# Group norms in the stage ahead, an image's chunks loaded as they are last read, two tiles' weighing on VectorE and smaller clears, in a four-layer image network

## The chip, the cores and the metric

The kernel runs on one core of a Trainium2 chip. The metric is the device time of one execution in microseconds (us). Engines are named as in the profile: PE is TensorE (PEld its weight loads), DVE VectorE, ACT ScalarE, POOL GpSimd, and SP the engine that issues most DMAs.

## The reference, cut to what matters

Four images of 56 x 56 positions and 128 channels go through four layers. Each layer takes the group-normed image (32 groups of 4 channels, statistics over all positions of one image) and adds its result to the image.

```python
x = x + L0(group_norm(x))   # window attention (7x7 windows, shifted by 3) + full attention + MLP
x = x + L1(group_norm(x))   # mamba: projection, 3x3 conv, selective scan in four directions, gated output
x = x + L2(group_norm(x))   # deformable 3x3 convolution
x = x + L3(group_norm(x))   # as L0, other weights
```

So nothing of a layer can start on an image before the last position of the layer ahead of it is known: the norm's statistics need them all. Different images are independent of one another.

## The kernel before, in words

An image is held as a tile of 128 channels (partitions) by 3136 positions, in seven chunks of 448. Two such tiles, `xs[b % 2]`, hold the images at work; image b+2 is loaded over image b when b is finished. `run` sets the order of the stages:

- b=0: attention L0(0), its MLP and the mamba convolution, scan(0), `mamba_out`(0);
- b=1: attention L0(1), MLP and convolution (1) woven with the deformable layer of image 0, scan(1), `mamba_out`(1), then attention L3(0) and `mlp` L3(0);
- b=2: the same with L0(2), deformable(1), `mamba_out`(2), L3(1);
- b=3: L0(3), deformable(2), `mamba_out`(3), attention L3(2), `mlp` L3(2) woven with deformable(3), and last attention L3(3) and `mlp` L3(3).

Statistics of chunk c (`stats`, line 124) are made on DVE as the chunk gets its final value, and `group_norm` (lines 142 to 159) turns them into a mean and 1/deviation for each channel: an aggregate on DVE (L146), a matmul that averages groups (gn_pm, L148), three small DVE operations, a second matmul (gn_pv, L155), a square root on ACT with a load of its function table (L157), and a reciprocal on DVE (L158).

An attention has two parts. The windows part works on eight bands of eight windows each, called tiles. For tile t, `tokens` (L241 to L249) gathers the band into xw, normed, in three to six pieces (on DVE for the first two tiles, on POOL for the others); `project` makes pq and pk on PE (L254); `queries`, `keys` and `values` bring them to qp, kb and v on ACT; `scores` makes pss on PE (L279) and takes the maximum away on DVE (L285, L286); `exponentials` is on ACT; `normalize` sums and inverts on DVE and multiplies to pz on POOL (L297, one product for each half of the partitions); `turn`, `turned`, `weigh` and `out` follow on PE and ACT. xw, qp, kb and pz exist twice and have padding that must be zero, so POOL clears them whole once in each attention (L243 and L249). The order of these steps, tile by tile, is written by hand. The main part, full attention over 3136 positions, follows it (maxima, L371 to L376; scores, L552; exponentials, L553; values, L579) and needs three tiles that POOL clears once in an attention: the ends of ks and qs (L344, L345) and mx (L359).

`mlp` runs over the seven chunks, an iteration for each n, with steps of several chunks in each: `center` (a matmul, a square on ACT, and on POOL the sum that reads x for the last time, L690), `spread`, `scale`, `shift`, `hidden` (PE and Gelu on ACT), `result` (py, L717) and `store` (L721). In layer L3 the store writes into x, and `finish` (L1519 to L1523) sends that chunk out and then loads the next image's chunk into the same place:

```python
    def finish(self, b, x, cols):
        self.nc.sync.dma_start(self.out[b][:, cols], x[:, cols])
        if b + 2 < self.B:
            self.nc.sync.dma_start(x[:, cols], self.x_in[b + 2][:, cols])
```

The statistics of images 2 and 3 are all made at the head of `run`'s loop, those of image 1 in `mamba_out`(0), each behind image 0's of the same chunk.

`mamba_out` (from L1207) does the last steps of the mamba layer by chunk: the scan's result ya less its mean (L1222, L1229), squares, a root (Ln and Exp on ACT), the gate z from the normed image (L162, L1240), and pmo (L1267), which `store` (L1270) adds to x. Ahead of it POOL's last work is the scan's sum hs (L1135).

Of the kernel before, what the change touches and what calls it, by code (L numbers as in the profile page):

```python
# [10 lines left out]
F32 = mybir.dt.float32  # L11
# [3 lines left out]
ALU = mybir.AluOpType  # L15
# [4 lines left out]
P = 128  # L20
HW = 56
L = HW * HW
CH = 448
# [55 lines left out]
class _Net:  # L79
    def __init__(self, ctx, tc, x, packs, out):  # L80
        self.tc, self.nc, self.x_in, self.out, self.packs = tc, tc.nc, x, out, packs
        self.B = x.shape[0]
        nc = self.nc
        wp = ctx.enter_context(tc.tile_pool(name="weights", bufs=1))
        self.keep = wp
        self.w = {}
        self.xs = [wp.tile([P, L], F32, tag=f"x{i}", name=f"x{i}") for i in range(2)]
        for c in range(NCK):
            cols = slice(c * CH, (c + 1) * CH)
            nc.sync.dma_start(self.xs[0][:, cols], x[0][:, cols])  # L90
        for layer, queue in (("L0", nc.scalar), ("C", nc.scalar), ("L1", nc.sync), ("L3", nc.sync)):
            self.load(layer, wp, queue)
        c = self.w["C"]
        self.ident, self.gmat = c["ident"], c["gmat"]
        self.ones = {1: c["ones1"], 2: c["ones2"]}
        self.center = {1: (c["center1"],), 2: (c["center2"], c["others2"])}
        self.sel = wp.tile([P, KB], F32R, tag="sel", name="sel")
        nc.vector.memset(self.sel.bitcast(F32), 0.0)
        for h in range(NH):
            nc.vector.memset(self.sel[h * DK : h * DK + 2, :].bitcast(F32), 1.0)  # L100
        self.ident2 = wp.tile([64 + NX, NX], F32R, tag="ident2", name="ident2")
        nc.vector.memset(self.ident2.bitcast(F32), 0.0)
        for k in (0, 64):
            nc.vector.tensor_copy(self.ident2[k : k + NX, :], self.ident[:NX, :NX])
        self.all1 = wp.tile([P, P], F32, tag="all1", name="all1")
        nc.vector.memset(self.all1, 1.0)
        self.one32 = self.all1[:, :DK]
        self.eps = wp.tile([P, 1], F32, tag="eps", name="eps")
        nc.vector.memset(self.eps, 1e-5)
        self.any = wp.tile([P, 1], F32, tag="any", name="any")  # L110
        self.sts = [wp.tile([P, NCK, 6], F32, tag=f"gn_st{i}", name=f"gn_st{i}") for i in range(2)]
        self.dpool = ctx.enter_context(tc.tile_pool(name="tables", bufs=1, space=DRAM))


# [26 lines left out]
    def group_norm(self, b, sb, bank):  # L141
        nc = self.nc
        st = self.sts[b % 2]
        self.table_of(AF.Sqrt)
        mv = sb.tile([P, 2], F32, tag="gn_mv", name="gn_mv")
        nc.vector.bn_aggr(mv, st.rearrange("p c s -> p (c s)"))  # L146
        pm = bank("gn_pm")
        nc.tensor.matmul(pm[:, 0:1], lhsT=self.gmat, rhs=mv[:, 0:1], start=True, stop=True)  # L148
        mean = sb.tile([P, 1], F32, tag="gn_mean", name="gn_mean")
        nc.vector.tensor_copy(mean, pm[:, 0:1])  # L150
        dv = sb.tile([P, 1], F32, tag="gn_dv", name="gn_dv")
        nc.vector.tensor_sub(dv, mv[:, 0:1], mean)
        nc.vector.scalar_tensor_tensor(dv, dv, dv, mv[:, 1:2], ALU.mult, ALU.add)
        pv = bank("gn_pv")
        nc.tensor.matmul(pv[:, 0:1], lhsT=self.gmat, rhs=dv, start=True, stop=True)  # L155
        rstd = sb.tile([P, 1], F32, tag="gn_rstd", name="gn_rstd")
        nc.scalar.activation(rstd, pv[:, 0:1], AF.Sqrt, bias=self.eps)  # L157
        nc.vector.reciprocal(rstd, rstd)  # L158
        return mean, rstd

    def gn_apply(self, out, x, gn):
        self.nc.vector.tensor_scalar(out, x, gn[0], gn[1], ALU.subtract, ALU.mult)  # L162
# [58 lines left out]
    def windows(self, layer, x, x1, gn, sb, bank):  # L221
# [18 lines left out]

        def tokens(t):  # L241
            if t < 2:
                nc.gpsimd.memset(xw[t], 0.0)  # L243
            xv = xw[t % 2][:, :, :n1].rearrange("p w (r c) -> p w r c", c=WS)
            for (a, r, c), at in self.window_pieces(order[t]):
                (nc.vector if t < 2 else nc.gpsimd).tensor_scalar(xv[:, a, r, c], self.piece(img, at), gn[0], gn[1], ALU.subtract, ALU.mult)
            if t < 2:
                for z in (qp, kb, pz):
                    nc.gpsimd.memset(z[t], 0.0)  # L249

        def project(t):
            for n in "qk":
# [38 lines left out]
        def normalize(t):  # L291
            s, d = later.pop(("s", t)), later.pop(("m", t))
            nc.vector.tensor_reduce(d, s, AX.X, ALU.add)
            nc.vector.reciprocal(d, d)  # L294
            for j in range(2):
                rows = slice(64 * j, 64 * j + 64)
                nc.gpsimd.tensor_tensor(pz[t % 2][rows, :, j, :n1], s[rows], d[rows, :, None].to_broadcast([64, ng, n1]), ALU.mult)  # L297

        def turn(t):
            for r in range(NPR):  # L300
# [28 lines left out]
    def attention(self, layer, b, x1, oT, sb):  # L329
# [11 lines left out]
        qs = sb.tile([P, LP], F32, tag="qs", name="qs")  # L341
        nm = sb.tile([P, L], F32R, tag="nm", name="nm")
        va = sb.tile([P, NKB, P], F32, tag="va", name="va")
        nc.gpsimd.memset(ks[:, L:], 0.0)  # L344
        nc.gpsimd.memset(qs[:, L:], 0.0)  # L345

        def part(c):
            return slice(c * CH, (c + 1) * CH)
# [7 lines left out]
        size = {g[0]: len(g) for g in groups_of}  # L356
        early = (NCK, NCK, NCK, NCK, NCK - 1, 1)
        mx = sb.tile([P, len(blocks), NH, NMX], F32, tag="mx", name="mx")
        nc.gpsimd.memset(mx, -3.0e38)  # L359
        used = {}  # L360

        xn = oT
        with tc.manual_schedule():
# [35 lines left out]

            with tc.tile_pool(name="ap_sb", bufs=2) as tb, tc.tile_pool(name="ap_ps", bufs=8, space=PSUM) as ps:  # L400
                bank = lambda name: ps.tile([P, 512], F32, tag="mm", name=name)
                of_windows = self.windows(layer, x, x1, self.group_norm(b, tb, bank), tb, bank)
                self.table_of_both()
                ln = {}

# [51 lines left out]
                for name in ("tokens", "project", "queries", "keys", "values"):  # L457
                    do(name, 0)
                do("tokens", 1)
                for u in range(NWIN + 1):  # L460
                    if u != 1:
                        do("scores", u)
# [206 lines left out]
    def mlp(self, layer, b, x1, oT, last, alone):  # L669
# [3 lines left out]
        with tc.tile_pool(name="mlp", bufs=2) as sb, tc.tile_pool(name="mlp_ps", bufs=1, space=PSUM) as ps:  # L673
            bank = lambda name, tag="mm": ps.tile([P, 512], F32, tag=tag, name=name, bufs={"mm": 6 if alone else 3, "pc": 2 if alone else 1}[tag])
            x2, m = x1, {}

            def cols(n):
                c = (n + 3) % NCK
# [7 lines left out]
            def center(n):  # L686
                (m["pc", n],) = self.ln_center([x2[:, cols(n)]], lambda name: bank(name, "pc"))
                m["sq", n] = sb.tile([P, 2, CH], F32, tag="ln_sq", name="ln_sq")
                nc.scalar.activation(m["sq", n][:, 0, :], m["pc", n][:, :CH], AF.Square)
                nc.gpsimd.tensor_add(x2[:, cols(n)], x2[:, cols(n)], x[:, cols(n)])  # L690

            def spread(n):
                sq = m["sq", n]
# [24 lines left out]

            def store(n):
                del m["h", n]  # L720
                nc.vector.scalar_tensor_tensor(x[:, cols(n)], m.pop(("py", n))[:, :CH], w["b2"], x2[:, cols(n)], ALU.add, ALU.add)  # L721
                if last:
                    self.finish(b, x, cols(n))
                else:
                    self.stats(b, (n + 3) % NCK)

# [12 lines left out]
            for n in range(-1, NCK):  # L739
                if do(hidden, n, (0, 1)):  # L740
                    yield 1.8
                do(scale, n + 1)
                if do(center, n + 2):
                    yield 0.9
                if do(hidden, n, (2, 3)):
                    yield 1.8
                do(shift, n + 1)
                if do(residual, n + 4):
                    yield 0.9
                if do(spread, n + 2):  # L750
                    yield 0.9
                if do(result, n, (0, 1)):
                    yield 1.8
                if do(result, n, (2, 3)):
                    yield 1.8
                do(store, n)


    def mamba_prepare(self):
# [450 lines left out]
    def mamba_out(self, b, ya, gn):  # L1210
# [3 lines left out]
        with tc.tile_pool(name="mo", bufs=2) as sb, tc.tile_pool(name="mo_ps", bufs=8, space=PSUM) as ps, tc.manual_schedule():  # L1214
# [54 lines left out]
            def store(c):  # L1269
                nc.vector.tensor_add(x[:, part(c)], x[:, part(c)], m.pop(("po", c))[:, :CH])  # L1270
                self.stats(b, c)
                if b == 0:
                    self.stats(1, c)

            def do(f, c):
                if 0 <= c < NCK:
                    f(c)

            tokens(0)
            for c in range(-1, NCK + 1):  # L1280
                do(mean, c + 1)
                do(gated, c - 1)
                do(less, c + 1)
                do(scale, c)
                do(gate, c + 1)
                do(out, c - 1)
                do(tokens, c + 2)
                do(spread, c + 1)
                do(store, c - 1)


# [224 lines left out]
                                late.append((add, c))  # L1516
                    yield 1.2

    def finish(self, b, x, cols):  # L1519

        self.nc.sync.dma_start(self.out[b][:, cols], x[:, cols])
        if b + 2 < self.B:
            self.nc.sync.dma_start(x[:, cols], self.x_in[b + 2][:, cols])  # L1523

    def first_half(self, b, s1, mb, made, alone):

        yield from self.mlp("L0", b, *made["at"], False, alone)
# [9 lines left out]
    def run(self):  # L1537
# [5 lines left out]
        self.nc.sync.dma_start(self.xs[1], self.x_in[1])  # L1543
        self.deform_prepare()
        for b in range(self.B):
            if b > 1:
                for c in range(NCK):
                    self.stats(b, c)
            with ExitStack() as mb:
                s1, made = ExitStack(), {}  # L1550
                made["at"] = self.swin_attention("L0", b, s1)
# [96 lines left out]
```

## Time and profile before

| what | value |
| --- | --- |
| three runs | 12027.29, 12049.42, 12027.54 us; median 12027.54 |
| the profiled execution | 12027.19 us, of which the span of the profile is 12025.4 |
| eight main parts of the attentions | 535.5 or 540 us each, 4302 in all |
| four scans | about 1000 us each |
| last pmo of `mamba_out` to the first pq of the attention behind it | 9.9 us for L0(1); 5.9 us, three times, for L3(0) to L3(2) |
| last py of `mlp` L3(0) or L3(1) to the first pq of L0(2) or L0(3) | about 11.2 us each |

The profile is of one execution. Lines of the timeline give the start and the duration of an operation (or of several alike, with their number behind the x), its engine, its line in the kernel, what it writes and reads, and in brackets how long its engine had been idle and what ended that. Matmuls go slower where the chip grants PE a lower clock (PEclk, a share of full speed).

### The profile page before, as it was taken

What the parts mean: (1) busy time and instruction counts of PE and PEld (TensorE: products, weight loads), DVE (VectorE), ACT (ScalarE), POOL (GpSimd) and SP (SyncE); (2) the same over time, 40 slices, a digit from 0 to 9 for tenths busy, and PEclk for the clock granted to TensorE, in tenths of its full rate; (3) what the DMA queues carried; (4) which work ended last, traced back from release to release, by engine and by line L of the source; (5) the groups of instructions that cost most, each with busy time, mean ns of one, the idle gap of its engine ahead of it and who ended that gap; (6) DMA issues with size and microseconds to landing.
All of it is one profiled execution on the core that took longest, in us unless ns stands there. A gap on an engine that the chain in (4) does not pass through costs nothing.

```text
span 12025.4 us, 221470 instructions
## 1 busy us (share of the span) xinstructions
PE 10887.6 (91%) x86844; PEld 7134.5 (59%) x86844; DVE 9107.5 (76%) x11751; ACT 8070.4 (67%) x21127; POOL 9481.8 (79%) x5876
## 2 busy tenths in 40 slices
PE   8998998998899899999889989999988998997799
PEld 4538886544688755454468865545447886553454
DVE  6749997766899877476689987747568997774575
ACT  5677776567777656656777765665677776567566
POOL 5949995796899759479689975948878996697497
PEclk9999999998899999999889999999989999998899
DMA  1000000005100000000610000000061000004200
GB/s 66 2 12 8 5 5 1 1 1 168 56 6 5 2 1 2 12 1 3 176 47 5 5 2 1 1 12 1 11 180 35 5 5 2 1 2 145 68 2 7
DMA packets 146308, 321.21 MB, mean 27 GB/s; under 512 B 17980, under 2 KB 87664, under 8 KB 145136
## 3 DMA queue, kind: packets, MB, share of 16 engines
q0 software_dynamic: 70848, 231.27, 6.6%
q1 hardware_dynamic: 74128, 74.57, 2.0%
q8 instruction: 687, 11.26, 0.4%
q14 instruction: 357, 2.92, 0.1%
q10 hardware_dynamic: 288, 1.19, 0.0%
HBM read 259.05 MB, written 47.90 MB: 26 GB/s over the span
## 4 chain that ended last, share of the span: by engine, by line
PE 59%; DVE 13%; POOL 13%; ACT 10%; issue 3%; DMA 1%; DVEq 0%; POOLq 0%; ACTq 0%; SPq 0%
PE pm L371 15%; PE po L579 10%; POOL hs L1135 10%; DVE hs L1126 8%; PE pst L552 7%; PE pst L543 3%; PE pd L568 2%; PE yt L1144 2%; PE pyb L1165 2%; PE dbu L1108 2%; PE pc L822 1%; DVE dgb L1012 1%; PE pvt L1469 1%; DVE mx L376 1%; POOL du L1058 1%
## 5 line engine op out<-in xcount | busy, mean ns | idle before, releaser
L376 DVE TENSOR_REDUCE mx<-pm 128x1 f32<-128x512 f32 (+7 forms) x6424 | 3376.8, 560 | 998.3 <-PE pm L371 920.8
L563 POOL TENSOR_TENSOR es<-es,e 128x896 f32<-128x896 f32 x1824 | 3764.2, 2090 | 77.9 <-ACT e L553 29.9
L1126 DVE TENSOR_TENSOR_SCAN hs<-da,dbu 128x928 f32<-128x928 f32 x1792 | 3618.2, 2069 | 34.3 <-ACT dbu L1119 19.1
L553 ACT ACTIVATE e<-pst 128x448 f32<-128x448 f32 (+1 forms) x5600 | 2592.7, 549 | 1531.0 <-PE pst L552 1096.4
L1135 POOL TENSOR_TENSOR hs<-hs,cb 128x896 f32<-128x896 f32 x1792 | 3434.5, 1949 | 20.4 <-ACT carry L1130 18.3
L371 PE MATMUL pm<-ks,qs 32*128 32x448 f32 (+5 forms) x12848 | 2965.2, 528 | 13.3 <-DVE nm L397 7.8
L552 PE MATMUL pst<-qs,ks 32*128 32x448 f32 x11200 | 2324.3, 539 | 0.0
L371 PEld LDWEIGHTS pm<-ks,qs 32*128 32x128 f32 x12848 | 1280.9, 187 | 1119.4 <-DVE mx L376 621.8
L1144 PE MATMUL yt<-w_C,hs 128*116 128x128 f32 x14336 | 1877.5, 274 | 16.6 <-POOL hs L1135 15.1
L543 PE MATMUL pst<-nm,sel 32*128 32x448 f32 x5600 | 1666.8, 527 | 6.9 <-DVE nm L397 6.9
L1144 PEld LDWEIGHTS yt<-w_C,hs 128*116 128x116 f32 x14336 | 1567.6, 135 | 43.7 <-POOL hs L1135 32.9
L1108 PE MATMUL dbu<-dgb,ut 112*128 112x224 f32 x7168 | 1250.6, 297 | 202.2 <-DVE hs L1126 199.1
L579 PE MATMUL po<-e,va 128*32 128x448 f32 (+1 forms) x11200 | 1358.4, 554 | 0.0
L1334 POOL DMA_INDIRECT g<-tab,idx x900 | 954.4, 1060 | 437.8 <-issue 228.8
L552 PEld LDWEIGHTS pst<-qs,ks 32*128 32x128 f32 x11200 | 1253.9, 187 | 1.6
L1063 ACT ACTIVATE da<-dl,A 128x112 f32<-128x112 f32 x3584 | 1193.4, 382 | 0.1
L1108 PEld LDWEIGHTS dbu<-dgb,ut 112*128 112x128 f32 x7168 | 949.1, 193 | 321.3 <-DVE hs L1126 309.5
L543 PEld LDWEIGHTS pst<-nm,sel 32*128 32x128 f32 x5600 | 710.9, 185 | 164.5 <-issue 145.5
L1130 ACT COPY carry<-hs 128x32 f32<-128x32 f32 x1792 | 396.2, 221 | 548.3 <-DVE hs L1126 527.8
L297 POOL TENSOR_TENSOR pz<-s,m 64x784 f32<-64x784 f32 x128 | 191.8, 1498 | 679.3 <-DVE m L294 674.8
L579 PEld LDWEIGHTS po<-e,va 128*32 128x32 f32 (+1 forms) x11200 | 222.6, 108 | 825.2 <-issue 763.5
L1080 PE MATMUL pt<-w_C,dh 128*112 128x128 f32 x3584 | 552.2, 278 | 151.3 <-DVE dgb L1012 145.2
(227 smaller groups left out, 14586.4 us busy)
## 6 DMA issues: line engine op xcount, KB each, us to landing
g<-tab,idx POOLq DMA_INDIRECT x900, 3.7
tab<-zero SPq DMA_DIRECT2D x4, 3364.0 KB
dl_d<-dl SPq DMA_DIRECT2D x28, 448.0 KB
dl<-dl_d SPq DMA_DIRECT2D x56, 224.0 KB
tab<-gt SPq DMA_DIRECT2D x16, 448.0 KB
out_dram<-x SPq DMA_DIRECT2D x28, 224.0 KB
tab<-gt SPq DMA_DIRECT2D x16, 336.0 KB
x<-in_x_dram SPq DMA_DIRECT2D x21, 224.0 KB
```

What stands on the lines that cost most here:

```text
L371: nc.tensor.matmul(pm[:, at : at + m], lhsT=qs[head(h), q : q + P], rhs=ks[head(h), keys], start=True, stop=True)
L376: nc.vector.tensor_reduce(mx[:, i, h, n : n + 1], p, AX.X, ALU.max)
L543: nc.tensor.matmul(pst[g, h][:, :CH], lhsT=self.sel[head(h), :], rhs=nm[head(h), part(g // NKB)], start=True, stop=False)
L552: nc.tensor.matmul(t[:, :CH], lhsT=ks[head(h), k * KB : (k + 1) * KB], rhs=qs[head(h), part(qc)], start=False, stop=True)
L553: nc.scalar.activation(es[g, p][:nk, j, :], t[:nk, :CH], AF.Exp, scale=SCALE)
L563: nc.gpsimd.tensor_tensor(s, es[g - 1, p][:nk] if k == 1 else s, es[g, p][:nk], ALU.add)
L579: nc.tensor.matmul(m["po"][head(h), :CH], lhsT=va[:nk, k, head(h)], rhs=src(h)[:nk], start=(k == 0), stop=(k == NKB - 1))
L1063: nc.scalar.activation(m["da"][:, :, n, 2:], dl(), AF.Exp, scale=A[:, j, n : n + 1])
L1108: nc.tensor.matmul(pu[:, 8 * h : 8 * h + 8, 2 + tb * TB : 2 + (tb + 1) * TB], lhsT=made[g]["ut", 2 * r + tb][:, d, :], rhs=made["r", g // ...
L1126: nc.vector.tensor_tensor_scan(flat(pairs[u // 2][:, d % 2]), flat(made[g]["da"][:, r]), flat(banks.pop(u)), 0.0, ALU.mult, ALU.add)
L1135: nc.gpsimd.tensor_tensor(hs, hs, made["r", g // 2]["cb"][:, :, r * HW : (r + 1) * HW], ALU.mult)
L1144: nc.tensor.matmul(sums[q][:YR, e * P : (e + 1) * P], lhsT=hs[:, n, :], rhs=self.ident, start=(n == 0), stop=(n == NST // 2 - 1), is_trans ...
```

## The change

Five edits:

1. `early_norm` does `group_norm`'s steps in two halves, inside the stage ahead, into tiles of its own; the attention takes what it finds in `ready`. For L0(1) and L3(0) to L3(2) the halves stand in `mamba_out` at c=3 and c=4; for L0(2) and L0(3) in the last iteration of `mlp` L3(0) and L3(1), before and behind the second half of `hidden`. It uses Ln and Exp in place of the square root. L0(0) and L3(3) keep `group_norm`.
2. In `mlp` L3, `store` writes into a tile of its own, xo (two buffers), and that is sent out; the next image's chunk is loaded right behind `center`'s last reading of x, and its statistic is made one iteration later.
3. The statistics of image 1 in `mamba_out`(0) are made two by two in the first four iterations.
4. `normalize`'s two products for tiles 0 and 1 go to DVE.
5. xw and qp are cleared in their padding alone (128 x 8 x 15 instead of 128 x 512), and the clears of ks, qs and mx move to behind the second tile's tokens in the order written by hand. By that order POOL's clears for an attention behind `mamba_out` no longer wait for its last matmul, and stand right behind the scan's last hs.

```diff
+    def early_norm(self, layer, b, bank, step, load=False):
+        nc = self.nc
+        mv, mean, dv, rstd = self.norms[b % 2]
+        if step == 0:
+            nc.vector.bn_aggr(mv, self.sts[b % 2].rearrange("p c s -> p (c s)"))
+            pm = bank("gn_pm")
+            nc.tensor.matmul(pm[:, 0:1], lhsT=self.gmat, rhs=mv[:, 0:1], start=True, stop=True)
+            nc.vector.tensor_copy(mean, pm[:, 0:1])
+            nc.vector.tensor_sub(dv, mv[:, 0:1], mean)
+            nc.vector.scalar_tensor_tensor(dv, dv, dv, mv[:, 1:2], ALU.mult, ALU.add)
+        else:
+            pv = bank("gn_pv")
+            nc.tensor.matmul(pv[:, 0:1], lhsT=self.gmat, rhs=dv, start=True, stop=True)
+            if load:
+                self.table_of_both()
+            self.one_over_root(rstd, pv[:, 0:1])
+            self.ready[layer, b] = mean, rstd
...
         def tokens(t):
             if t < 2:
-                nc.gpsimd.memset(xw[t], 0.0)
+                nc.gpsimd.memset(xw[t][:, :, n1:], 0.0)
...
             if t < 2:
-                for z in (qp, kb, pz):
-                    nc.gpsimd.memset(z[t], 0.0)
+                for z in (kb[t], qp[t][:, :, n1:], pz[t]):
+                    nc.gpsimd.memset(z, 0.0)
...
-                nc.gpsimd.tensor_tensor(pz[t % 2][rows, :, j, :n1], s[rows], d[rows, :, None].to_broadcast([64, ng, n1]), ALU.mult)
+                on = nc.vector if t < 2 else nc.gpsimd
+                on.tensor_tensor(pz[t % 2][rows, :, j, :n1], s[rows], d[rows, :, None].to_broadcast([64, ng, n1]), ALU.mult)
...
-        nc.gpsimd.memset(ks[:, L:], 0.0)
-        nc.gpsimd.memset(qs[:, L:], 0.0)
...
-        nc.gpsimd.memset(mx, -3.0e38)
...
-                of_windows = self.windows(layer, x, x1, self.group_norm(b, tb, bank), tb, bank)
+                of_windows = self.windows(layer, x, x1, self.ready.pop((layer, b), None) or self.group_norm(b, tb, bank), tb, bank)
...
                 do("tokens", 1)
+                nc.gpsimd.memset(ks[:, L:], 0.0)
+                nc.gpsimd.memset(qs[:, L:], 0.0)
+                nc.gpsimd.memset(mx, -3.0e38)
... mlp:
+            following = last and b + 2 < self.B
                 nc.gpsimd.tensor_add(x2[:, cols(n)], x2[:, cols(n)], x[:, cols(n)])
+                if following:
+                    nc.sync.dma_start(x[:, cols(n)], self.x_in[b + 2][:, cols(n)])
...
-                nc.vector.scalar_tensor_tensor(x[:, cols(n)], m.pop(("py", n))[:, :CH], w["b2"], x2[:, cols(n)], ALU.add, ALU.add)
+                made = sb.tile([P, CH], F32, tag="xo", name="xo") if last else x[:, cols(n)]
+                nc.vector.scalar_tensor_tensor(made, m.pop(("py", n))[:, :CH], w["b2"], x2[:, cols(n)], ALU.add, ALU.add)
                 if last:
-                    self.finish(b, x, cols(n))
+                    nc.sync.dma_start(self.out[b][:, cols(n)], made)
...
+                if following and n == NCK - 1:
+                    self.early_norm("L0", b + 2, bank, 0)
                 if do(hidden, n, (2, 3)):
                     yield 1.8
+                if following and n == NCK - 1:
+                    self.early_norm("L0", b + 2, bank, 1, True)
...
                 do(store, n)
+                if following and n + 1 < NCK:
+                    self.stats(b + 2, (n + 4) % NCK)
... mamba_out:
                 self.stats(b, c)
-                if b == 0:
-                    self.stats(1, c)
...
+            following = ("L3", b - 1) if b > 0 else ("L0", 1)
             for c in range(-1, NCK + 1):
+                if b == 0:
+                    for k in (2 * c + 2, 2 * c + 3):
+                        if k < NCK:
+                            self.stats(1, k)
...
                 do(spread, c + 1)
+                if c in (3, 4):
+                    self.early_norm(*following, bank, c - 3)
                 do(store, c - 1)
... run:
-            if b > 1:
-                for c in range(NCK):
-                    self.stats(b, c)
```

More of the change, by code (lines that the diff above doesn't have):

```diff
@@ L111, in __init__ @@
         self.sts = [wp.tile([P, NCK, 6], F32, tag=f"gn_st{i}", name=f"gn_st{i}") for i in range(2)]
+        self.ready = {}
+        self.norms = [[wp.tile([P, n], F32, tag=f"gn_{i}{j}", name=f"gn_early{i}") for j, n in enumerate((2, 1, 1, 1))] for i in range(2)]
         self.dpool = ctx.enter_context(tc.tile_pool(name="tables", bufs=1, space=DRAM))
@@ L1517, in deform @@
                     yield 1.2
[L1519 to L1523, printed above, removed]
     def first_half(self, b, s1, mb, made, alone):
```

## The prediction

> **What bounds the kernel.** The page comes first: its busy row, then its chain of waits.
>
> ```profile
> PE 10887.6 (91%) x86844; PEld 7134.5 (59%) x86844; DVE 9107.5 (76%) x11751; ACT 8070.4 (67%) x21127; POOL 9481.8 (79%) x5876
> ...
> PE 59%; DVE 13%; POOL 13%; ACT 10%; issue 3%; DMA 1%; DVEq 0%; POOLq 0%; ACTq 0%; SPq 0%
> ```
>
> No engine bounds the whole: the attentions' main parts run on PE, the scans on POOL (L1135) and DVE (L1126). The change touches neither, only the seams between stages and the first two tiles of each windows part. A seam is serial, so I read three in the timeline (start, duration, engine, line; in brackets the idle time before and what ended it). First mlp L3(0) to L0(2):
>
> ```profile
> 4975.23 0.68 DVE L721 SCALAR_TENSOR_TENSOR x<-py,w_L,x 128x448 f32<-128x448 f32 x1 [0.16 <-PE py L717]
> ...
> 4977.92 0.33 SPq L1523 DMA_DIRECT2D x<-in_x_dram  x1
> 4980.36 0.63 DVE L126 BATCH_NORM_STATS2 gn_st<-x 128x6 f32<-128x448 f32 x1 [4.45 <-DMA x<-in_x_dram]
> ...
> 4983.51 1.28 ACT L157 ACT_TABLE_LOAD   x1 [10.72 <-PE gn_pv L155]
> ...
> 4985.29 1.67 DVE L246 TENSOR_SCALAR xw<-x,gn_mean,gn_rstd 128x343 f32<-128x343 f32 x6
> ...
> 4986.32 1.64 PE L254 MATMUL pq<-xw,w_L 128*128 128x392 f32 x2 [2.90 <-DVE xw L246]
> ```
>
> The last chunk goes out, the next image's comes in behind it (L1523 waits for L1521's transfer, issued at 4975.94), and only then do statistics, norm and tokens follow: 11.1 us from py's end (4975.12) to pq. Next, mamba_out(1) to L3(0), and below the "..." mamba_out(0) to L0(1):
>
> ```profile
> 4189.15 0.62 DVE L1270 TENSOR_TENSOR x<-x,pmo 128x448 f32<-128x448 f32 x1 [3.44 <-PE pmo L1267]
> 4189.18 0.15 POOL L344 MEMSET ks<- 128x64 f32 x1 [65.83 <-PE pmo L1267]
> ...
> 4193.55 3.37 DVE L246 TENSOR_SCALAR xw<-x,gn_mean,gn_rstd 128x343 f32<-128x343 f32 x6
> ...
> 4195.06 1.65 PE L254 MATMUL pq<-xw,w_L 128*128 128x392 f32 x2 [3.45 <-DVE xw L246]
> ...
> 1999.15 4.03 DVE L246 TENSOR_SCALAR xw<-x,gn_mean,gn_rstd 128x343 f32<-128x343 f32 x6 [0.46 <-DVE gn_rstd L158]
> ...
> 2002.54 1.64 PE L254 MATMUL pq<-xw,w_L 128*128 128x392 f32 x2 [5.68 <-DVE xw L246]
> ```
>
> Here the norm is in the way as well, and POOL's clears: ks (L344) waited 65.83 us for mamba_out's last matmul, so the large clears behind it run while DVE makes tokens, and the six pieces take 4.03 and 3.37 us instead of 1.67.
>
> **The change, part by part.** Times are of the profiled execution: 12027.19, of which the span is 12025.4; the median of the three runs is 12027.54.
>
> A, mamba_out(0) to L0(1). What stays behind the last pmo (end 1992.64) is the residual add 0.62, one statistic 0.6 that the program's order leaves between the pieces, the first tile's three pieces 0.83 (half of 1.67) and a handover of 0.2: pq at 1994.9 instead of 2002.54. Gain 7.6.
>
> B, mamba_out(b) to L3(b-1), three times: 4189.15 + 0.62 + 0.6 + 0.83 + 0.2 = 4191.4 instead of 4195.06; 7180.93 to 7186.84 and 10166.05 to 10171.92 are the same pattern. Gain 3.65 each, 10.9.
>
> C, mlp L3(0) and L3(1) to the next L0. The transfers leave the path: each chunk's load goes out behind center's POOL add, and the statistic is made an iteration later. In its place the norm's steps enter the mlp's last iteration: gn_pm waits there for the store before it (0.68), its statistic (0.63) and the aggregate (0.34), with PE's matmuls of hidden queued behind; I take 0.55 of stall, 0.4 for gn_pm and 0.45 for gn_pv (rows 0.56 and 0.59 at half clock): the tail is 1.4 longer. The table load (1.28) lies behind the last Gelu (4973.75) and Ln and Exp after it end at about 4975.5, before py does. So py ends at 4976.5, the store by 4977.3, pq starts at 4977.4. Gain 8.9 each (the second, to 7973.05, has the same rows), 17.8.
>
> The clock after C: PE now idles under 1 us. In this profile pq, pk take 1.64 a pair behind the seam and 0.82 to 0.93 each at full clock, and kb(0) begins 3.05 after pq where 1.6 would do: 1.4 each, 2.8. Behind A and B I count nothing; up to 1.4 each goes into the range.
>
> D, mlp L3(2) to L3(3), keeps its norm; its pieces no longer meet the clears: 1.1.
>
> Weighing of two tiles on DVE: 0. The windows read:
>
> ```profile
> 4205.51 2.36 ACT L264 ACTIVATE kb<-pk,w_L 32x392 f32<-32x392 f32 x4
> ...
> 4206.14 3.07 POOL L297 TENSOR_TENSOR pz<-s,m 64x784 f32<-64x784 f32 x2 [3.84 <-DVE m L294]
> ...
> 4208.90 0.57 DVE L285 TENSOR_REDUCE m<-pss 128x8 f32<-128x392 f32 x1 [2.94 <-PE pss L279]
> ```
>
> The pair takes 3.07 on POOL. DVE's nearest row is a 128x768 product (L1458) at 0.95, so 1.9 a pair (bounds 1.2 and 3.0). It fits DVE's idle 2.94 before 4208.90. PE's scores(1) starts at 4207.98, when ACT's kb ends (4207.87), not on pz (4209.21); so an earlier pz moves nothing before the turn, which waits in PE's queue behind those scores. If the cover is gone, L285 and with it exponentials(1) shift by the excess.
>
> Costs. POOL's clears now run from the last hs add (4123.4) for some 8.2 us, beside mamba_out's start:
>
> ```profile
> 4128.94 0.50 DVE L162 TENSOR_SCALAR xg<-x,gn_mean,gn_rstd 128x448 f32<-128x448 f32 x1
> ...
> 4130.88 1.16 DVE L1229 TENSOR_TENSOR xc<-pm,ya 128x448 f32<-128x448 f32 x2 [1.45 <-PE pm L1222]
> ```
>
> The two clears of pz (1.8) and the second kb end between 4130.6 and 4131.6; a piece of xw that met them took 2.84 where 0.48 is usual, so L162 may end only then and L1229 start 0 to 1.1 late. I take 0.6, four times: 2.4 (bounds 0 and 2.5 each).
>
> The Trainium skill, "SBUF — State Buffer", section on the two sides, has VectorE and GpSimd hold their shared port for a whole instruction, exclusively; the 2.84 agrees. It speaks against moving both clears and products, and by it alone the cost would be the whole 2.5 each, a forecast 7.6 later.
>
> The early norm's Ln and Exp on ACT: 0.25 each (sqrt's row 0.26), less 0.2 of ACT's idle time: 0.3, four times 1.2. DVE's wait for gn_pm at c=3 delays less(c+2) by 1.9, which its squares' slack covers: 0. The smaller clears save POOL time that nobody waits for: 0. The first attention has one more table load, on an idle ACT: 0.
>
> Sum: 7.6 + 10.9 + 17.8 + 2.8 + 1.1 - 2.4 - 1.2 = 36.6. From 12027.2 to 11990.6; at the median, 11990.9 (0.30% down). About 0.2%, 24 us, can be told from no change here.
>
> **The rivals.** The largest term outside the seams is the granted clock (the last but one column of the stretch table, behind each engine's busy time):
>
> ```profile
> 4372.00:4912.00 540.00, 538.24 (x5222) 259.56 (x5223) 372.65 (x723) 339.16 (x743) 505.78 (x248) 0.99 0.01 1
> 7363.00:7899.00 536.00, 534.24 (x5226) 258.42 (x5223) 372.76 (x723) 339.46 (x744) 505.73 (x248) 1.00 0.01 2
> 4840.00:4856.00 16.00, 14.24 (x90) 4.58 (x87) 1.04 (x2) 7.62 (x19) 8.94 (x5) 0.68 0.00 1
> 4978.00:4992.00 14.00, 5.92 (x18) 4.26 (x20) 3.34 (x12) 5.99 (x9) 0.85 (x1) 0.52 0.06 16
> ```
>
> The same work takes 540 us in one main part and 535.5 in another: five of the eight have 10.2 us at half clock near 4841, behind a short hole in PE, three have none. That is 4.6 each; clock changes stand on a grid of 3.41 us, so moving a seam by a few us can change which ones are hit.
>
> *Adverse clock:* all eight are hit, +13.8: 12004.7, within the bound. *Favourable clock:* none is, -23.0: 11967.9. The three runs of before within 0.4 us speak for a grid tied to the program's own start, against a lottery per run; I can't tell how a new phase falls.
>
> The Trainium skill, "TensorE: Matmul & The Clock Gate", section on what is actually happening, has a free-running window of about 3.4 us and halves the clock after an idle one; the grid of 3.41 agrees.
>
> *Slower:* the windows parts (PEclk 0.90 to 0.93) are dense with holes as long as the one at 4841. In a shifted phase more of them are judged idle. A half-clock stretch of 3.41 us costs up to 1.7; the gain is used up at 36.6/8/1.7 = 2.7 more in each of eight windows parts, and slower by over the bound begins at 4.5. With five each: 68 us, 12058.9. Against it: eight windows parts already start at eight phases and show about the same clock.
>
> *The product waits:* POOL's tokens(3) (2.48) sits at 4204.6 to 4207.1 and may hold up DVE's products, so that they end past 4208.90. At 1.6 in each attention, 12.8: 12003.7.
>
> *The change doesn't close seams A and B:* another step is late there (rstd on ACT behind mamba_out's Silu, or clears still beside the tokens), and only C and D gain: 36.6 - 18.5 = 18.1: 12009.4.
>
> **How the numbers follow.** Forecast 0.66: its seams are serial rows. Favourable 0.06, adverse 0.07, product 0.05, seams A and B 0.06, slower 0.10, the sum of small risks I can't see in this trace put on that mechanism. Faster: 0.66 + 0.06 = 0.72; within the bound 0.07 + 0.05 + 0.06 = 0.18; slower 0.10. Low end: gain 36.6, full clock behind A and B 5.6, two main parts less at half clock 9.2, no clears' cost 2.4: 53.8, 11974. High end: less the clears' bound 7.6 and three more main parts 13.8: 15.2, 12012. This leaves out the favourable and the slower case, 0.16.
>
> **What would show it.** Right: pq (L254's matmul) 2.3 us after the last pmo at the four mamba seams and 2.3 after py's end at the two mlp seams, no DMA and no L126 between; POOL's clears right behind the last hs; the two DVE products done before L285; main parts of 540 and 536 us in some new mixture. Wrong: gn_pm stalling PE for several us in the mlp's last iteration; L162 of 2 us or more with the chain of mamba_out behind it; L285 of tile 1 waiting for DVE's product; main or windows parts longer at lower PEclk.

## The result, and the profile after

The changed kernel takes 12002.55 us (median of 8 runs, 11989.09 to 12009.23), the one before 12043.89 (8 runs, 12027.29 to 12053.93): a ratio of 0.9971 with a 95% interval of 0.9963 to 0.998. The profiled executions differ by less: spans 12025.4 and 12003.7, 21.7 apart.

The stages by their first and last matmuls, in both profiles (us):

| stage | before | after | difference |
| --- | --- | --- | --- |
| last pmo to first pq of L0(1) | 9.90 | 3.91 | -5.99 |
| the same to L3(0), L3(1), L3(2) | 5.94 to 5.95 | 3.90 to 3.91 | -2.04 each |
| last py to first pq of L0(2), L0(3) | 11.20, 11.25 | 1.28 | -9.92, -9.97 |
| mlp L3(0), L3(1) | 62.99 | 63.94 | +0.95 each |
| first to last pmo, four times | 186.3 | 186.2 | -0.1 |
| windows parts of L0(2), L0(3) | 177.81, 177.78 | 176.27, 176.31 | -1.54, -1.46 |
| the six other windows parts | 1058.2 | 1062.0 | +3.7 |
| eight main parts (five at 540 in both) | 4307.7 | 4307.6 | -0.2 |

(By these limits a main part runs from its first po to its last, and before's eight come to 4307.7 us, not to the 4302 of the table ahead.) The seams give 32.0, and with the mlp's and the two windows' rows it is 33. The spans differ by 21.7 only, because after lost 11.5 us elsewhere: 3.7 in the other windows parts, 3.2 in the starts of `mamba_out`, some 5 in the stages woven with gathers. These rows differ as much between two profiles of one kernel: from the scan's last yt to the first pmo, `mamba_out`(0) takes 22.93, 19.37 and 18.15 us in the three profiles of after, and 19.73 and 18.15 in two of before.

The seam behind mlp L3(0), in the timeline of after:

```profile
4964.06 0.38 PE L171 MATMUL gn_pm<-gn_early,w_C 128*128 128x1 f32 x2 [0.24 <-DVE gn_early L169]
...
4966.74 1.28 ACT L136 ACT_TABLE_LOAD   x1
...
4968.57 1.27 DVE L268 TENSOR_SCALAR xw<-x,gn_early,gn_early 128x343 f32<-128x343 f32 x4 [3.48 <-ACT gn_early L141]
4969.75 0.67 DVE L748 SCALAR_TENSOR_TENSOR xo<-py,w_L,x 128x448 f32<-128x448 f32 x1
...
4970.57 0.90 PE L276 MATMUL pq<-xw,w_L 128*128 128x392 f32 x2 [1.28 <-DVE xo L748]
```

The norm costs PE 0.24 of waiting, the table load stands beside the py matmuls, and the first tile's tokens are done within 0.2 us of py's end (4969.29). What is left is the store, 0.46 late behind the second tile's first piece, and a handover; pq runs at full clock (0.90 for two, where 1.64 was). Now mamba_out(1) to L3(0):

```profile
4183.26 0.62 DVE L1303 TENSOR_TENSOR x<-x,pmo 128x448 f32<-128x448 f32 x1 [3.45 <-PE pmo L1300]
4183.34 0.20 POOL L265 MEMSET xw<- 128x120 f32 x1 [65.92 <-PE pmo L1300]
4183.47 1.40 POOL L271 MEMSET kb<- 128x1568 f32 x1
4183.80 1.29 DVE L268 TENSOR_SCALAR xw<-x,gn_early,gn_early 128x343 f32<-128x343 f32 x1
...
4185.13 1.80 POOL L271 MEMSET pz<- 128x2048 f32 x1
4185.54 3.12 DVE L268 TENSOR_SCALAR xw<-x,gn_early,gn_early 128x28 f32<-128x28 f32 x5
...
4187.13 1.65 PE L276 MATMUL pq<-xw,w_L 128*128 128x392 f32 x2 [3.90 <-DVE xw L268]
```

The norm is gone from the path, but POOL's clears are not at mamba_out's start: the first one had waited 65.92 us, for the last pmo as before. So they still run beside the tokens; the first piece takes 1.29 and not 0.48, the next five 3.12.

### The profile page after: what moved, and what is told of

Same layout as the page of the kernel before. It is cut to its first block, busy times and chain, and to the rows that moved or that the text cites. A ratio compares the mean times of both kernels' runs of the same rounds, so it can differ in the third digit from the quotient of the medians.

```text
span 12003.7 us, 221429 instructions
## 1 busy us (share of the span) xinstructions
PE 10899.7 (91%) x86844; PEld 7143.4 (60%) x86844; DVE 9140.9 (76%) x11777; ACT 8056.3 (67%) x21118; POOL 9437.3 (79%) x5844
## 4 chain that ended last, share of the span: by engine, by line
PE 59%; DVE 14%; POOL 12%; ACT 10%; issue 4%; DMA 1%; DVEq 0%; POOLq 0%; ACTq 0%; SPq 0%
PE pm L391 15%; PE po L602 10%; DVE hs L1159 10%; POOL hs L1168 8%; PE pst L575 7%; PE pst L566 3%; PE pd L591 2%; PE yt L1177 2%; PE pyb L1198 2%; PE dbu L1141 2%; PE pc L855 1%; DVE dgb L1045 1%; DVE mx L396 1%; POOL du L1091 1%; PE pvt L1507 1%
## 5 line engine op out<-in xcount | busy, mean ns | idle before, releaser
L586 POOL TENSOR_TENSOR es<-e 128x896 f32<-128x896 f32 x112 | 231.7, 2090 | 560.3 <-ACT e L576 560.3
```

The source lines that it names most:

```text
L586: nc.gpsimd.tensor_tensor(s, es[g - 1, p][:nk] if k == 1 else s, es[g, p][:nk], ALU.add)
```

## The experiments

Theory: the gain is the sum of the seams, the weighing costs nothing, and what is left behind mamba_out is the clears. Rivals: luck of the clock; a gain or a loss elsewhere, in the weighing, in mamba_out or in the mlp. The first four kernels ran on one chip (before: 12043.53, 21 runs); before_a, before_b, pz_on_pool and tokens_first on a second (before: 12120.07, 13 runs); the four timed last on a third (before: 12121.39, 16 runs). On the second and third every kernel is slower, so each ratio is to before on the same chip. The seams agree on all three to 0.2 us; it is the stages woven with the deformable layer's gathers that take longer there (from the last py of the mlp to the scan's first yt 254 to 255 us in before, 262 to 267 in before_a), and not the scans (3980.0 and 3980.5 us in all).

**after_again**, the changed kernel unedited.

> The changed kernel once more. Theory (the seams): the stages between the attentions repeat to 0.2 us, so the six changed seams take 3.9, 3.9, 3.9, 3.9, 1.3 and 1.3 us again and the profiles differ in the main and windows parts alone, by 4.6 us a main part and 1.4 us a windows part; time 0.997 of before (0.9963 to 0.998). Rival (luck): most of the gain is the granted clock of the runs that were drawn, and a second set of runs gives 0.998 or more, with the eight main parts as long as before's.

Measured: 11990.22 (11978.01 to 12003.97), ratio 0.9959 (0.9945 to 0.9972). The six seams are 3.91, 3.91, 1.29, 3.91, 1.29, 3.91; five main parts take 540 again, but other ones. The luck rival falls: the gain is there in a second set. It is 53 us there, 20 more than the rows; where these 20 come from is not shown.

**mamba_only**, of the change the norms in `mamba_out` alone (and the earlier statistics of image 1):

```diff
+            following = ("L3", b - 1) if b > 0 else ("L0", 1)
             for c in range(-1, NCK + 1):
...
                 do(spread, c + 1)
+                if c in (3, 4):
+                    self.early_norm(*following, bank, c - 3)
```

> Before, with the early norms in mamba_out alone (clears, loads and weighing as before). Theory (the clears are what is left in these seams): the whole clear of xw now comes ahead of the first piece and kb and pz beside the others, so pq starts 4.5 to 5.9 us after the last pmo, in place of 9.9 and 5.9 before and 3.9 after: 5 us from L0(1), 0 to 1.4 from each of the three others, 5 to 9 us in all (0.9993 to 0.9996). Rival (the norm was all there was in the way): 2.3 us at all four, 18 us, 0.9985. The seams behind mlp L3 stay at 11.2.

Measured: 0.9982 (0.9973 to 0.9991). The four seams take 3.73, less than the 4.5 to 5.9 expected and less than after's 3.91: 6.2 from L0(1), 2.2 from each other, 12.8 in all. Both sizes were missed: the norm was not all that was in the way (2.3), and the large clears stand no worse than the small ones.

**mlp_only**, of the change the early load, xo and the norms in `mlp` alone:

```diff
                 nc.gpsimd.tensor_add(x2[:, cols(n)], x2[:, cols(n)], x[:, cols(n)])
+                if following:
+                    nc.sync.dma_start(x[:, cols(n)], self.x_in[b + 2][:, cols(n)])
...
+                if following and n == NCK - 1:
+                    self.early_norm("L0", b + 2, bank, 0)
```

> Before, with the early load, xo and the early norms in mlp L3 alone. Theory: the two seams take 1.3 us in place of 11.2, the mlp 1.0 longer, the windows part behind 1.5 shorter by the clock: 2 x 10.4 = 21 us, 0.9983. Rival (PE's wait for the norm's steps and the chunk's transfers give it back): the mlp 3 us or more longer, and 0.9990 or more. The seams behind mamba_out stay at 9.9 and 5.9.

Measured: 0.9974 (0.9965 to 0.9983). Seams 1.29 and 1.28, mlp 63.95, windows parts 1.5 shorter, the mamba seams 9.90 and 5.95 as before: the theory's rows, and nothing given back. The times of this kernel and the last (31 and 22 us under before) lie above their rows (21 and 12.8), within the intervals.

**old_clears**, after with before's clears:

```diff
-                nc.gpsimd.memset(xw[t][:, :, n1:], 0.0)
+                nc.gpsimd.memset(xw[t], 0.0)
...
-                for z in (kb[t], qp[t][:, :, n1:], pz[t]):
-                    nc.gpsimd.memset(z, 0.0)
+                for z in (qp, kb, pz):
+                    nc.gpsimd.memset(z[t], 0.0)
...
+        nc.gpsimd.memset(ks[:, L:], 0.0)
+        nc.gpsimd.memset(qs[:, L:], 0.0)
...
+        nc.gpsimd.memset(mx, -3.0e38)
...
-                nc.gpsimd.memset(ks[:, L:], 0.0)
-                nc.gpsimd.memset(qs[:, L:], 0.0)
-                nc.gpsimd.memset(mx, -3.0e38)
```

> After, with the clears as before (whole xw and qp, ks, qs and mx first). Theory: the seams behind mamba_out take 4.5 to 5.9 us in place of 3.9, so the smaller clears and their place are worth 0.6 to 2 us at each of four seams, 2 to 8 us; behind mlp L3 nothing changes (1.3), since POOL is idle there long before. Rival (the place of the clears is nothing): 3.9 at the four seams.

Measured: 0.9955 (0.9941 to 0.9968), against 0.9959 of after beside it. The mamba seams take 3.73 instead of 3.91, and at L3(3) it is 7.13 from the last x to pq instead of 7.56. So the edit of the clears brings nothing; by these rows it costs 1.1 us (0.4 of it at L3(3), a row that pz_on_pool below shows to be unsteady). The timeline shows why it could not be worse:

```profile
4185.35 0.15 POOL L367 MEMSET ks<- 128x64 f32 x1 [65.88 <-PE pmo L1300]
...
4186.31 0.53 POOL L265 MEMSET xw<- 128x512 f32 x1
4186.78 0.53 POOL L271 MEMSET qp<- 128x512 f32 x1
4186.87 1.99 DVE L268 TENSOR_SCALAR xw<-x,gn_early,gn_early 128x343 f32<-128x343 f32 x3 [0.26 <-POOL xw L265]
```

Both kernels wait for the same pmo. Here the three pieces come out with one collision (1.99), in after with two.

**before_a** and **before_b**, the kernel before, profiled twice more.

> The kernel before, once more, for a second profile of it. Theory (the clock is drawn for each execution): the seams repeat to 0.1 us (9.9, 5.9, 11.2), while other main parts than in the first profile take 540 us in place of 535.5; the sum of the eight differs by a multiple of 4.6. Rival (the clock follows the program): the same five main parts of eight take 540.

> The kernel before, a third profile: as before_a. Over the profiles of all kernels 33 of 48 main parts so far took 540; if the timed runs of before (median 12043.5) are slower than its first profile (12027.2) for this reason, six to eight of eight take 540 here.

Measured: 12121.07 and 12127.43. Seams 9.90, 5.95, 11.3 again. Six and four of the eight main parts take 540, in before_a L0(0), L3(0), L0(2), L3(1), L0(3) and L3(2), in before_b L0(0), L3(0), L3(1) and L3(3). The clock is drawn in each execution, and so is the place of its grid: from the program's first instruction to the grid's next step it is 1.14, 0.20 and 3.19 us in the three profiles of before. That before's first profile (12027.19) was a lucky one against its median fits, but more parts at half clock in typical executions are not seen here.

**pz_on_pool**, after with all weighing on POOL:

```diff
-                on = nc.vector if t < 2 else nc.gpsimd
-                on.tensor_tensor(pz[t % 2][rows, :, j, :n1], s[rows], d[rows, :, None].to_broadcast([64, ng, n1]), ALU.mult)
+                nc.gpsimd.tensor_tensor(pz[t % 2][rows, :, j, :n1], s[rows], d[rows, :, None].to_broadcast([64, ng, n1]), ALU.mult)
```

> After, with the weighing of all tiles on POOL again. Theory (it was hidden): the first turn starts 14.4 us after pq at full clock, with either engine; nothing at the seams changes (3.9 and 1.3) and the time is that of after, 0.9955 to 0.997 of before. Rival (the product waits, or is late on POOL): the first turn moves by 1 us or more in each of eight windows parts, 8 us or more in all, 0.0007.

Measured: 0.997 (0.9958 to 0.9981). In L0(2) and L0(3), at full clock, the first turn starts 14.33 after pq, with DVE 14.34 and in mlp_only (POOL) 14.34. The timeline of after (L3(0), the product on DVE), and then of this kernel (L0(2), on POOL):

```profile
4198.14 1.96 DVE L320 TENSOR_TENSOR pz<-s,m 64x784 f32<-64x784 f32 x2
...
4201.66 0.57 DVE L307 TENSOR_REDUCE m<-pss 128x8 f32<-128x392 f32 x1 [1.56 <-PE pss L301]
```
```profile
4996.52 3.07 POOL L319 TENSOR_TENSOR pz<-s,m 64x784 f32<-64x784 f32 x2 [4.28 <-DVE m L316]
...
4998.36 2.88 PE L301 MATMUL pss<-kb,qp 128*64 128x196 f32 x16 [3.40 <-POOL pz L319]
...
5001.17 3.04 PE L325 MATMUL pt<-w_C,pz 128*128 128x128 f32 x13
```

The product takes 1.96 or 3.07 and is done (4200.10, 4999.59) before the scores that stand ahead of the turn in PE's queue are through (4202.93, 5001.24); DVE is idle for 1.56 after it. The releaser named for pss, pz, is the first of the two products (done at 4998.02); kb ends later (4998.26), and pss follows kb by 0.1 with either engine.

One row moved that was expected to stay: at L3(3) pq comes 8.92 us behind the start of the last x, and not 7.56. POOL's clears stand at the same places there to 0.01 us, but the first piece of tokens takes 3.62 instead of 0.77. That a difference of hundredths decides which clears a piece has to let pass is inferred; but D's small loss can't be read as a price of the edit. By the time, this kernel is 33.7 us under before, and 13.8 over tokens_first on the same chip, of which the seams' rows explain 10.3; after itself was not timed on that chip.

**tokens_first**, after with the pad strips first, and the large clears behind the first tile's tokens (at L0(1) and all L3):

```diff
-            if t < 2:
-                nc.gpsimd.memset(xw[t][:, :, n1:], 0.0)
+            if t == 0:
+                for z in xw + qp:
+                    nc.gpsimd.memset(z[:, :, n1:], 0.0)
...
+        behind = layer == "L3" or b == 1
...
+            if t == 0 and behind:
+                nc.gpsimd.tensor_copy(sb.tile([P, 1], F32, tag="seen", name="seen", bufs=1), xw[0][:, NWIN - 1, n1 - 1 : n1])
             if t < 2:
-                for z in (kb[t], qp[t][:, :, n1:], pz[t]):
+                for z in (kb[t], pz[t]):
```

> After, with the two tiles' pad strips of xw and qp cleared first, and a POOL copy of one element of the last token piece ahead of the clears of kb and pz, so that these start behind the first tile's tokens (for L0(1) and all L3). Theory (the large clears lengthen the pieces by 1.6 us): pq 2.3 us after the last pmo in place of 3.9, four times, and 0.7 to 1.4 us less between norm and pq at L3(3): 7 to 8 us less than after, 0.9950 to 0.996 of before. Rival (kb or pz is then cleared too late): qp, kb or the first turn waits for POOL and the windows part grows by as much.

The same kernel was timed a second time beside after; that run carries the label tokens_filled.

> The kernel tokens_first again (clears of kb and pz behind the first tile's tokens; no idle matmuls in this one), to be timed on the same chip as after. Theory: seams of 2.1 us behind mamba_out, 7 us for the four, and 1.8 at L3(3): 8 to 9 us less than after. Rival (given back in the windows parts): the time of after.

Measured: 0.9965 (0.9951 to 0.9978), and the second time 0.9965 (0.9953 to 0.9977), with after at 0.9962 (0.9948 to 0.9976) beside it. By the rows the theory holds: 2.13 at all four mamba seams, and 5.78 instead of 7.56 at L3(3).

```profile
4191.88 0.48 DVE L270 TENSOR_SCALAR xw<-x,gn_early,gn_early 128x343 f32<-128x343 f32 x1
...
4193.36 0.31 POOL L272 COPY seen<-xw 128x1 f32<-128x1 f32 x1 [1.32 <-DVE xw L270]
4193.44 0.90 PE L280 MATMUL pq<-xw,w_L 128*128 128x392 f32 x2 [2.13 <-DVE xw L270]
4193.61 1.39 POOL L275 MEMSET kb<- 128x1568 f32 x1
...
4195.24 2.37 ACT L290 ACTIVATE kb<-pk,w_L 32x392 f32<-32x392 f32 x4 [0.22 <-PE pk L280]
```

The first piece is back at 0.48 and kb is cleared (4195.00) in time for ACT, so nothing waits for POOL there. Nor is it given back later as far as the profiles show: the five windows parts concerned come to 883.7 and 886.3 us in its two, and to 881.2 to 885.8 in after's three. The gain is 1.78 x 5, or 9 us of rows; the timed runs (12074.14, 12062.45 to 12097.5, against 12073.36 of after) can't tell it from nothing. Seven main parts took 540 in one of its profiles and four in the other, 14 us apart.

**before_filled** and **after_filled**, with matmuls that nobody reads in two waits of PE late in each main part:

```diff
                 pt = bank("pmt")
+                for _ in range(3 if i == 23 else 0):
+                    nc.tensor.matmul(pt[:, 256:512], lhsT=self.ident, rhs=qs[:, :256], start=True, stop=True)
...
                     pst[g, h] = bank("pst")
+                    for _ in range(2 if (g, h) == ((NCK - 1) * NKB, 0) else 0):
+                        nc.tensor.matmul(pst[g, h][:, :CH], lhsT=self.ident, rhs=qs[:, :CH], start=True, stop=True)
```

> Before, with idle matmuls (nobody reads them) in PE's two waits of 0.9 us some 471 and 473 us into each main part. Theory (those two waits 0.4 us apart are what the clock is halved for, when its grid falls so): all eight main parts take 535.3 to 536 us, 4285 in all in place of 4303 to 4317; time 20 to 28 us under before, 0.9977 to 0.9983. Rival (the half clock comes from elsewhere, or moves to the next hole): some main parts still take 540, and the time is that of before.

> After, with the same idle matmuls. Theory: 0.995 x before again less 20 to 28 us; against before_filled it is a cleaner comparison of the two kernels, since the main parts no longer differ: the seams' sum, 32 us, and 3 by the clock behind the mlp's seams, less 3 of the longer mlp: 30 to 35 us. Rival (there is a gain that the seams don't have, as the runs of parts of the change suggest): 45 us or more against before_filled.

Measured: 0.9981 (0.9972 to 0.999) and 0.9955 (0.9942 to 0.9969). Of the 16 main parts in the two profiles none takes 540: all lie between 536.2 and 537.1. The stretch tables, of after (a main part, and 16 us around the two waits of the next one) and of before_filled (a main part, and 16 us around its waits):

```profile
4365.00:4905.00 540.00, 538.25 (x5220) 260.16 (x5221) 372.77 (x723) 338.99 (x743) 505.69 (x248) 0.99 0.01 1
...
5616.00:5632.00 16.00, 14.24 (x92) 4.40 (x90) 1.04 (x2) 8.25 (x19) 8.87 (x5) 0.68 0.00 0
```
```profile
5171.00:5707.50 536.50, 536.50 (x5233) 260.11 (x5231) 372.81 (x723) 339.53 (x744) 506.08 (x248) 1.00 0.01 2
...
5640.00:5656.00 16.00, 16.00 (x141) 6.20 (x138) 1.04 (x2) 11.06 (x26) 11.40 (x6) 1.00 0.01 1
```

Filling the 1.76 us that PE was idle there takes the half clock away (0.68 to 1.00); it costs 0.9 where the part would have taken 535.5. So the 4.6 us are these two waits. The filling does not end the scatter, though: before_filled's 11 runs lie within 24.8 us, the 16 of before beside them within 31.9.

And the cleaner comparison: after_filled (12069.36) is 32.4 under before_filled (12101.78), what the seams' rows say and not 45 or more, though with runs that spread over 12 and 25 us. The rival of a gain beyond the seams falls in this pair; it is not settled for the unfilled kernels, where the medians differ by 41 to 53 us.

**after_c**, the changed kernel timed beside them.

> The changed kernel, timed on this chip beside the others: 30 to 45 us under before, main parts of 535.5 and 540 mixed as before, 20 to 28 us over after_filled.

Measured: 12073.36 (12067.94 to 12085.64), 48 us under before and 4 over after_filled, where 20 to 28 were expected. That is open. The filling was worth 20 to before and 4 to after; by 4.6 a part, and 0.9 paid in each of eight, before's timed runs would have had 5.8 parts at half clock and after's 2.4, yet after's three profiles show five each.

## Why the prediction was right or wrong

The forecast was 36.6 us less; the medians differ by 41.3 and the rows by 32.7. By its own terms:

| term | forecast | measured in the rows |
| --- | --- | --- |
| A, mamba_out(0) to L0(1) | 7.6 | 6.0 |
| B, three seams to L3 | 10.9 | 6.1 |
| C, two seams behind mlp L3, less the longer mlp | 17.8 | 18.0 |
| the clock behind C | 2.8 | 3.0 |
| D, L3(3) | 1.1 | -0.4 |
| clears beside mamba_out's start | -2.4 | 0 |
| Ln and Exp in mamba_out | -1.2 | 0 |
| weighing on DVE | 0 | 0 |
| sum | 36.6 | 32.7 |

Right: C, to 0.1 a seam, though its parts were not (the seam before is 11.20 us and not the 11.1 read there; the mlp grew by 0.95 where 1.4 stood, as gn_pm made PE wait 0.24 and not 0.55); the clock behind it, where the first pss starts 4.16 after pq instead of 5.56; and the weighing, by the reason given, the scores ahead of the turn in PE's queue. pz ended 1.56 before DVE was next needed, so the rival in which the product waits has no place.

The step that failed is "POOL's clears now run from the last hs add (4123.4)"; the fifth edit's description says the same. In the program the first clear, xw's, carries a wait for mamba_out's last product and last pmo: these semaphores stand in instructions of their own ahead of the clear, and reading the clear alone misses them. The trace of after has them on the clear's line (L265): POOL waits there till 4179.86 and then till 4183.27, 0.05 us behind the last product and 0.04 behind the last pmo. Taking ks, qs and mx away from the head of POOL's queue therefore only handed the wait to xw. The step cost the sum 1.6 of gain a seam at A and B (6.4 in all, shown by tokens_first, which has 2.13), and 2.4 were charged to mamba_out that nobody paid: at full clock its start takes 18.15 us in both kernels. The rival in which seams A and B don't close named "clears still beside the tokens"; it came true in part, for A and B still gained 12.1.

D failed by the clears too. There they start with the last x in both kernels (10.70 us of POOL's waiting in after), and with shorter clears ahead, the first tile's pieces met the second tile's clear of pz (to 11218.84) where before they met that of kb: 0.4 lost instead of 1.1 gained.

So the sum came near by errors that cancel: 7.9 too much in A, B and D, against 3.6 charged to mamba_out and not paid. That the medians differ by 41.3 is no support for it either, as the rows don't explain more than 32.7.

The Trainium skill, "SBUF — State Buffer", section on the two sides, lets the one of VectorE (in some of its operations) and GpSimd that starts first hold their shared port to the end of its instruction. The trace agrees: the piece of 0.48 beside strips takes 1.29 when a clear of 1.40 began ahead of it, and ends 0.2 behind that clear. The 2.5 a seam that the forecast drew from it for mamba_out did not come, since no clear was there.

A second step was wrong in its evidence: "The three runs of before within 0.4 us speak for a grid tied to the program's own start". Two of the three were within 0.3 us and the third 22 us above. Read rightly, they said that the clock is drawn in each execution, as before_a and before_b then showed. The profiled execution of before was 17 us below the median of before's eight runs, and the sum was made against it. The adverse, the favourable and the slower case were all costed as if a shifted seam would set the clock for good; in fact each execution draws anew (four to seven parts of eight at half clock in all unfilled profiles), so they are a part of the runs' scatter and not outcomes of the change. The slower case did not show: the windows parts differ by less than 0.1% in all.

## What to carry to other kernels

A clear at the head of an engine's queue can wait for the whole stage ahead (here for 65.9 us, presumably because its tile takes that stage's memory; no run shows the reason); moving it up does nothing until that wait is found, also where it stands in a separate instruction ahead. Work that is moved off a seam is worth what the next latest thing leaves of it: look at what runs beside it, and put large clears behind the operation that they slow, with a small read as the order. Where single executions scatter by more than the change is worth, cost the change by rows that repeat to 0.2 us, and where a cause of the scatter is known, remove it in both kernels before comparing their times.

## What the runs showed of the hardware

Two waits of PE of 0.9 us each, 0.4 us apart, can be enough to halve its clock for 10.2 us. In the profile of before, in steps about as long as the clock's grid (3.41 us), but not on it:

```profile
4840.00:4843.00 3.00, 2.32 (x20) 0.85 (x17) 0.00 (x0) 2.54 (x7) 2.92 (x2) 1.00 0.00 0
4843.00:4846.40 3.40, 2.32 (x14) 1.02 (x14) 0.41 (x1) 0.49 (x2) 3.17 (x2) 0.74 0.00 0
4846.40:4849.80 3.40, 3.40 (x23) 0.61 (x19) 0.00 (x0) 2.28 (x5) 0.00 (x0) 0.50 0.02 5
4849.80:4853.20 3.40, 3.40 (x24) 1.06 (x20) 0.62 (x1) 1.10 (x3) 0.05 (x1) 0.50 0.00 0
```

PE is busy for 2.32 of 3.00 and 2.32 of 3.40 us there, and then stays at 0.50 through stretches in which it is never idle.

Whether a main part is hit depends on where the grid lies. In the clock records of the twelve unfilled profiles the changes stand on a grid of 3.41 us; laid over PE's two waits, it gives for each of the 96 main parts the most idle time that one step holds. In the 64 parts of 540 us it is 1.34 to 1.76 us, in the 32 others 0.88 to 1.34, with the border between 1.336 and 1.344 in all of them: about 39% of a step. So the draw is the grid's place, and a hole that fits into one step counts for more than the same hole across two.

The Trainium skill, "TensorE: Matmul & The Clock Gate", section on what is actually happening, ties the low clock to an idle window of 3.4 us. Here no such window was idle: the idle time is 1.76 us in all, 1.34 of it in one step was enough to lose the clock, and filling it was enough to keep it. The measurement decides.
